# A decoder with routed experts on one Trainium2 core: smaller expert blocks, weights kept in SBUF, and a matrix read at a register's offset

## The chip, the cores and the metric

One core of a Trainium2 chip runs the whole program. Its engines work side by side, each through its own queue in order: TensorE (PE: matmuls, with the loading of the stationary operand shown as PEld), VectorE (DVE), ScalarE (ACT), GpSimd (POOL), and SyncE (SP), which here issues most DMAs. Work passes between them through SBUF and PSUM and is ordered by semaphores. The metric is the device time of one execution in microseconds (us). The trace comes from one profiled execution; its span runs from the first to the last instruction.

## What is computed

A two-layer decoder over 32 sequences of 128 tokens with 128 features, all fp32: 4096 tokens. Only the last step of layer 1 is touched, a mixture of 8 experts of which each token uses the two best:

```python
H, F, E, TOPK = (128, 512, 8, 2)
logits = xf @ router_w + router_b
probs = jax.nn.softmax(logits, axis=-1)
topk_w, topk_i = jax.lax.top_k(probs, TOPK)
topk_w = topk_w / jnp.sum(topk_w, axis=-1, keepdims=True)
...
h = jax.nn.relu(jnp.einsum('th,ehf->tef', xf, w1) + b1)
y = jnp.einsum('tef,efh->teh', h, w2) + b2
out = jnp.einsum('te,teh->th', gates, y)
```

The result is added to the residual stream. Before it come attention, cross attention and gated experts (layer 0), then causal attention and a latent cross attention (layer 1).

## The kernel before

**Order of work.** The program writes the order out by hand as a plan of *schedule slots*. `at(slot, phase, fn)` puts a piece of work in a slot; inside a slot the phases run as open, pre, the attention matmuls, inner, mid, post. Each attention stage takes two slots for each of its 32 sequences, so the three stages fill slots 0 to 191 and end some slots later; `done(stage, g)` is `8 * (8 * stage + g) + 17`, the slot after group g (four sequences) of that stage is finished. Work beside attention is planned relative to it. Each engine gets its instructions in the order of this plan; the sequencers of the engines run through them independently.

**Tokens to slots of a table.** Tokens are treated in two halves (groups 0 to 3 and 4 to 7) of 2048 tokens, 4096 token-expert pairs each. The router (`plan_route`, L1500 to 1690) handles units of eight or four sequences: it normalizes, computes logits on PE (L1571), picks two experts on DVE, counts ranks with matmuls (L1616, L1618), and POOL scatters one row of 130 numbers for each of the two choices (features, the token's row number, its gate) with indirect DMAs (L1644) into a DRAM table `slots[f]` in which each expert has its own room. The last unit is group 7 alone: eight scatters, two in each of slots 230 to 233.

**Blocks.** `expert_blocks` cuts the table of a half into `NB` blocks of `BLOCK` rows of one expert each. The number is fixed: `NB = 2 * HALF // BLOCK + E - 1`, that is 16 + 7 = 23 blocks of 256, whatever the router chooses. `table` (L1735 to L1760, DVE) works out for each block its expert's row in the weights and its first row in the table. For block j:

- `fetch_w` (L1764 to L1769): SP loads the weight row number into a register and issues one DMA of 514 KB, the block's expert's w1, w2 and b1, into one of four buffers `w`.
- `fetch_x` (L1773 to L1778): the same for the block's 256 rows, two to a partition (1040 bytes), into one of ten buffers `bx`.
- `turn`: two PE transposes (L1786) and a DVE copy (L1788) into `bxT`.
- `hidden`: four fp32 products of 256 columns (L1796; each product is two instructions), then bias and relu, two parts on ACT (L1804), two on DVE (L1806).
- `result`: eight fp32 products of 128 columns (L1813), scaled by the gates on ACT (L1821) and DVE (L1823).
- `leave`: two indirect DMAs on POOL (L1828) scatter the rows into `y`, two rows per token.

The order in slot s of block j is: transposes of j + 1, hidden of j, result of j - 1, then the fetches of x for j + 5 and of w for j + 3; the scatter of j - 2 stands between. Half 0's first block is in slot 211 and its last in slot 233, half 1's first in slot 236. In slots 203 to 230 the last groups of the latent attention and the router run beside the blocks; `lkv` (L1098, SP) fetches one sequence's keys each.

**Finish.** `gather` (L1841) reads two rows per token of `y` back, in two DMAs of 256 KB per group, rows of 512 bytes; `finish` adds them on POOL (L1845) and adds the residual on DVE (L1846); `store` (L1485) writes the output. For half 0 this happens beside half 1's blocks, for half 1 after the last block.

At the very end all engines load one word into a register (L1991) to decide whether a general path is needed, which is not taken with these inputs.

Of the kernel before, what the change touches and what calls it, by code (L numbers as in the profile page):

```python
# [22 lines left out]
P = 128  # L23
B, S, D = 32, 128, 128
DC = 96
NG = 4
# [9 lines left out]
ROOM, BLOCK = HALF, 256  # L36
# [3 lines left out]
W_ROW = 512 + 512 + 4  # L40
# [47 lines left out]
def constants():  # L88
# [8 lines left out]
    token = np.tile(np.arange(2 * HALF, dtype=np.int32).reshape(2, B // 2, P).transpose(2, 0, 1), (1, 1, 2))  # L97
# [11 lines left out]
def decoder(ctx: ExitStack, tc: tile.TileContext, a: dict, out: bass.AP):  # L109
# [1054 lines left out]
    def rest_general(y_att, y_mean, flag):  # L1164


        with tc.tile_pool(name="genw", bufs=1) as gw, tc.tile_pool(name="genr", bufs=2) as gp, tc.tile_pool(name="gens", bufs=2) as gs:
# [276 lines left out]
            def relu(x):  # L1444
# [6 lines left out]
                for e in range(E):  # L1451
                    pg = bank(ps_t)
                    nc.tensor.matmul(pg, pick_one[:, e, :], gT, start=True, stop=True)
                    for c in range(4):
                        ph = bank(ps_s)
                        nc.tensor.matmul(ph, w_f[:, e, c * P : (c + 1) * P], xT, start=True, stop=True)
                        h = t([P, NG * P], "fh", 2)
                        nc.scalar.activation(h, ph, AF.Relu, bias=w_f[:, e, 1024 + c : 1025 + c])
                        nc.vector.tensor_tensor(h, pg, h, ALU.mult)
                        nc.tensor.matmul(  # L1460
                            po, w_f[:, e, 512 + c * P : 512 + (c + 1) * P], h, start=False, stop=(e == E - 1 and c == 3)
                        )
# [266 lines left out]
    def expert_blocks(f, total, lazy):  # L1729
# [5 lines left out]
        def table():  # L1735
# [16 lines left out]
            first = row([2, NB], "first")  # L1752
# [5 lines left out]
            nc.vector.tensor_scalar(first[:, 0, :], first[:, 0, :], float(E - 1), float(D), ALU.min, ALU.mult)  # L1758
            where.append(row([2, NB], "where", I32))
            nc.vector.tensor_copy(where[0], first)  # L1760

        def fetch_w(j):
            s = state.setdefault(j, {})
            at_w = nc.values_load(  # L1764
                where[0][:, 0, j : j + 1], engines=[SP], min_val=0, max_val=(E - 1) * D,
                skip_runtime_bounds_check_because="an expert's number, cut off above, by 128",
            )
            s["w"] = lazy["blocks"].tile([P, W_ROW], F32, tag="w", name="w", bufs=4)
            nc.sync.dma_start(s["w"], a["w_f"][bass.ds(at_w, P), :])  # L1769

        def fetch_x(j):
            s = state.setdefault(j, {})
            at_x = nc.values_load(  # L1773
                where[0][:, 1, j : j + 1], engines=[SP], min_val=0, max_val=SLOTS - BLOCK,
                skip_runtime_bounds_check_because="the block's first slot, by the counts of all tokens",
            )
            s["x"] = lazy["blocks"].tile([P, 2, ROW], F32, tag="x", name="bx", bufs=10)
            nc.sync.dma_start(  # L1778
                s["x"].rearrange("p s w -> p (s w)"), slots[f][bass.ds(at_x, BLOCK), :].rearrange("(p s) w -> p (s w)", s=2)
            )  # L1780

        def turn(j):
            s = state[j]
            ps = bank(ps_a)
            for c in range(2):
                nc.tensor.transpose(ps[:, c * P : (c + 1) * P], s["x"][:, c, :D], ident)  # L1786
            s["xT"] = lazy["blocks"].tile([D, BLOCK], F32, tag="xT", name="bxT", bufs=2)
            nc.vector.tensor_copy(s["xT"], ps[:, :BLOCK])  # L1788

        def hidden(j):  # L1790
            s = state[j]
            s["h"] = lazy["blocks"].tile([P, 4, BLOCK], F32, tag="h", name="bh", bufs=2)
            for k in range(2):
                ps = bank(ps_s)
                for c in range(2):
                    nc.tensor.matmul(  # L1796
                        ps[:, c * BLOCK : (c + 1) * BLOCK], s["w"][:, (2 * k + c) * P : (2 * k + c + 1) * P], s["xT"],
                        start=True, stop=True,
                    )
                for c in range(2):  # L1800
                    n = 2 * k + c
                    p, bias = ps[:, c * BLOCK : (c + 1) * BLOCK], s["w"][:, 1024 + n : 1025 + n]
                    if k == 0:
                        nc.scalar.activation(s["h"][:, n, :], p, AF.Relu, bias=bias)  # L1804
                    else:
                        nc.vector.tensor_scalar(s["h"][:, n, :], p, bias, 0.0, ALU.add, ALU.max)  # L1806

        def result(j):
            s = state[j]
            ps = bank(ps_t)  # L1810
            for u in range(2):
                for c in range(4):
                    nc.tensor.matmul(  # L1813
                        ps[:, u * P : (u + 1) * P], s["h"][:, c, u * P : (u + 1) * P],
                        s["w"][:, 512 + c * P : 512 + (c + 1) * P], start=(c == 0), stop=(c == 3),
                    )
            o = s["o"] = lazy["blocks"].tile([P, 2, D], F32, tag="o", name="bo", bufs=4)
            for u in range(2):
                gate = s["x"][:, u, D + 1 : D + 2]
                if u == 0:  # L1820
                    nc.scalar.activation(o[:, u, :], ps[:, u * P : (u + 1) * P], AF.Identity, scale=gate)  # L1821
                else:
                    nc.vector.tensor_scalar(o[:, u, :], ps[:, u * P : (u + 1) * P], gate, None, ALU.mult)  # L1823

        def leave(j):
            s = state.pop(j)
            for u in range(2):
# [256 lines left out]
```

## Time and profile before

| | us |
|---|---|
| median of four runs | 1225.43 |
| lowest and highest | 1221.38, 1226.85 |
| the profiled execution | 1229.21 |
| its span | 1227.4 |

Busy time of each engine in five stretches of the span (us):

| stretch | what runs | PE | DVE | ACT | POOL | granted PE clock | DMA share |
|---|---|---|---|---|---|---|---|
| 933 to 966 | last projections, latent attention, router | 27.80 | 23.32 | 14.53 | 25.17 | 0.79 | 0.38 |
| 966 to 1086 | half 0's blocks beside latent attention and router | 108.00 | 62.32 | 36.73 | 64.42 | 0.94 | 0.42 |
| 1086 to 1113 | end of half 0, last scatters, pause | 18.70 | 9.39 | 5.34 | 17.45 | 0.94 | 0.43 |
| 1113 to 1203 | half 1's blocks | 88.65 | 38.42 | 27.68 | 50.50 | 0.96 | 0.67 |
| 1203 to 1227 | gather, add, store | 0.36 | 3.12 | 0.37 | 8.42 | 0.55 | 0.48 |

How to read the profile's lines: in a timeline, each line has the start and the duration in us, the engine, the source line, the operation, output and inputs, partitions and shape, and the count of instructions merged into it; in brackets the idle time before it and what ended that. In a table by stretches, the columns are length, then busy time and count of PE, PEld, DVE, ACT and POOL, then the granted clock, the DMA share and GB/s. In the answer for one source line, each line has the queue, the operation, the count, and shortest, median and longest duration in ns; a "q" behind an engine's name is its queue's own instruction.

### The profile page before, as it was taken

The page shows a single profiled execution, that of the slowest core. Times are in us where ns is not written, and L with a number is a line of the kernel's source. Part 1 is how long each engine was busy: PE and PEld are TensorE (multiplying, and loading weights), DVE is VectorE, ACT ScalarE, POOL GpSimd, SP SyncE. Part 2 cuts the span into 40 slices and gives each one's busy share as a digit, 9 for nine tenths or more (in the row PEclk, how much of TensorE's full clock was granted, in tenths as well). Part 3 has the DMA queues.
Part 4 walks back from the last instruction along what each step waited for, and adds up shares of the span by engine and source line. Part 5 has one row for each costly group of instructions (what it writes and reads, how often), then busy time and mean ns, then how long its engine had stood idle before and what let it go on. Part 6 is the DMA issues. An engine that isn't in the chain of part 4 may idle for free.

```text
span 1227.4 us, 30561 instructions
## 1 busy us (share of the span) xinstructions
PE 1104.5 (90%) x11877; PEld 822.4 (67%) x11877; DVE 805.2 (66%) x2279; ACT 569.9 (46%) x1299; POOL 639.4 (52%) x911
## 2 busy tenths in 40 slices
PE   3999999999999999999998999989898898887992
PEld 1666666777766667666656666766676687777992
DVE  1578778887778676776676778776676564352441
ACT  2245555577655545545445655644453532321330
POOL 5455445534452454425546664654755456654663
PEclk8599989999999999999999999988987899898996
DMA  7803533002021101110120000001101444445774
GB/s 196 251 8 97 175 97 97 29 27 63 2 46 45 28 19 37 36 36 3 35 47 5 10 15 15 10 11 29 30 16 43 121 145 126 146 148 158 250 237 113
DMA packets 83081, 92.09 MB, mean 75 GB/s; under 512 B 14274, under 2 KB 70264, under 8 KB 82928
## 3 DMA queue, kind: packets, MB, share of 16 engines
q1 hardware_dynamic: 77936, 81.57, 23.2%
q0 software_dynamic: 4992, 8.48, 2.0%
q8 instruction: 96, 1.57, 0.5%
q14 instruction: 57, 0.47, 0.1%
HBM read 53.84 MB, written 38.01 MB: 75 GB/s over the span
## 4 chain that ended last, share of the span: by engine, by line
PE 57%; DVE 14%; POOL 11%; issue 7%; ACT 4%; DMA 4%; SPq 2%; another core or an unknown queue 1%; POOLq 0%; DVEq 0%; ACTq 0%
PE bank L561 15%; PE bank L589 6%; PE bank L1796 4%; DVE msc L564 3%; PE bank L1813 3%; PE bank L871 3%; PE bank L353 2%; POOL y L1828 2%; PE bank L530 2%; PE bank L1143 2%; POOL h L862 2%; DMA g<-spread 2%; PE bank L853 2%; PE bank L1117 1%; PE bank L418 1%
## 5 line engine op out<-in xcount | busy, mean ns | idle before, releaser
L572 ACT ACTIVATE e<-bank 128x512 f32<-128x512 f32 x384 | 207.9, 594 | 239.1 <-PE bank L561 233.1
L564 DVE TENSOR_REDUCE msc<-bank 128x4 f32<-128x512 f32 x384 | 246.3, 683 | 71.7 <-PE bank L561 69.9
L561 PE MATMUL bank<-kb,qz 32*128 32x256 f32 x1536 | 245.4, 418 | 14.4 <-DVE msc L564 14.4
L561 PE MATMUL bank<-qa,kb 32*128 32x128 f32 x3072 | 234.7, 290 | 0.5 <-ACT e L572 0.5
L561 PEld LDWEIGHTS bank<-kb,qz 32*128 32x128 f32 x1536 | 147.6, 192 | 83.9 <-issue 44.1
L561 PEld LDWEIGHTS bank<-qa,kb 32*128 32x128 f32 x3072 | 196.6, 192 | 2.6 <-ACT e L572 1.6
L1828 POOL DMA_INDIRECT y<-bo,bx x92 | 91.7, 996 | 85.9 <-ACT bo L1821 62.7
L575 POOL TENSOR_SCALAR_AFFINE_SELECT e<-e 128x512 f32<-128x512 f32 x128 | 79.6, 646 | 98.5 <-ACT e L572 98.4
L589 PE MATMUL bank<-e,vt 128*32 128x128 f32 x3072 | 127.2, 283 | 3.4 <-POOL e L575 3.1
L1796 PE MATMUL bank<-bxT,w 128*128 128x256 f32 x368 | 92.5, 394 | 3.3 <-issue 1.7
L1813 PE MATMUL bank<-w,bh 128*128 128x128 f32 x736 | 93.8, 282 | 1.2 <-issue 1.2
L1813 PEld LDWEIGHTS bank<-w,bh 128*128 128x128 f32 x736 | 91.1, 198 | 5.3 <-issue 3.8
L589 PEld LDWEIGHTS bank<-e,vt 128*32 128x32 f32 x3072 | 73.3, 110 | 29.3 <-POOL e L575 5.4
L1644 POOL DMA_INDIRECT slots<-rows,r_ati x64 | 63.3, 989 | 31.9 <-issue 16.9
L1796 PEld LDWEIGHTS bank<-bxT,w 128*128 128x128 f32 x368 | 68.9, 198 | 13.1 <-issue 3.0
L862 POOL TENSOR_TENSOR h<-h,g 128x512 f32<-128x512 f32 x30 | 37.6, 1270 | 71.4 <-DVE nm_st L774 35.4
L1806 DVE TENSOR_SCALAR bh<-bank,w 128x256 f32<-128x256 f32 x92 | 40.2, 479 | 41.8 <-PE bank L1796 30.3
L1821 ACT ACTIVATE bo<-bank,bx 128x128 f32<-128x128 f32 x46 | 16.9, 367 | 95.9 <-PE bank L1813 45.9
L1124 ACT ACTIVATE le<-bank,lmx 128x256 f32<-128x256 f32 x64 | 26.8, 471 | 72.1 <-DVE lmx L1123 62.1
L470 DVE SCALAR_TENSOR_TENSOR qa<-bank,head_rows,qz 128x128 f32<-128x128 f32 x192 | 57.6, 342 | 4.0 <-PE bank L462 3.9
L307 ACT ACTIVATE xn<-x,ln_nb,ln_rs 128x128 f32<-128x128 f32 x96 | 41.9, 489 | 38.9 <-POOL ln_nb L301 38.9
L1804 ACT ACTIVATE bh<-bank,w 128x256 f32<-128x256 f32 x92 | 38.5, 470 | 41.0 <-PE bank L1796 20.7
(312 smaller groups left out, 2271.6 us busy)
## 6 DMA issues: line engine op xcount, KB each, us to landing
w<-in_w_f SPq DMA_DIRECT2D x46, 514.0 KB
slots<-nowhere SPq DMA_DIRECT2D x8, 2340.0 KB
g<-spread SPq DMA_DIRECT2D x16, 512.0 KB
bx<-slots SPq DMA_DIRECT2D x46, 130.0 KB
kv<-kcv SPq DMA_DIRECT2D x8, 516.0 KB
lkv<-kv SPq DMA_DIRECT2D x32, 129.0 KB
y<-y SPq DMA_DIRECT2D x16, 256.0 KB
x<-in_x SPq DMA_DIRECT2D x8, 256.0 KB
```

Source lines behind the costliest of these rows:

```text
L307: nc.scalar.activation(m["xn"][:, i, :], X[g][:, i, :], AF.Identity, scale=m["rs"][:, i : i + 1], bias=m["nb"][:, i : i + 1])
L470: nc.vector.scalar_tensor_tensor(s["qa"][:, u, :], s["mp"][:, :P], head_rows[:, 1 - u : 2 - u], m["qz"][:, u, i * P : (i + 1) * P], ALU.mu ...
L561: nc.tensor.matmul(o, l, r, start=start, stop=stop, skip_group_check=True)
L564: nc.vector.tensor_reduce(tops(MSC[bb % 4], 2 * h + j), sc[j].rearrange("p (s n k) -> p s n k", s=2, n=2), AX.X, ALU.max, negate=True)
L572: nc.scalar.activation(e.rearrange("p n q -> p (n q)"), tr[j], AF.Exp, scale=SCALE)
L575: nc.gpsimd.affine_select(out=e, in_=e, compare_op=ALU.is_ge, fill=0.0, base=0, pattern=[[0, 4], [1, P]], channel_multiplier=-1)
L589: nc.tensor.matmul(s3["av"][32 * n : 32 * n + 32, h3 * P : (h3 + 1) * P], m3["vt"][:, i3, h3, n, u, :], es[u][:, n, :], start=(h3 == 0 and ...
L862: engine.tensor_tensor(m["h"][:, c, :], m["h"][:, c, :], m["g"][:, c, :], ALU.mult)
L1644: ins = nc.gpsimd.indirect_dma_start(slots[f], bass.IndirectOffsetOnAxis(ap=m["ati"][:, c, n : n + 1], axis=0), m["rows"][c][:, n, :], Non ...
L1796: nc.tensor.matmul(ps[:, c * BLOCK : (c + 1) * BLOCK], s["w"][:, (2 * k + c) * P : (2 * k + c + 1) * P], s["xT"], start=True, stop=True,)
L1813: nc.tensor.matmul(ps[:, u * P : (u + 1) * P], s["h"][:, c, u * P : (u + 1) * P], s["w"][:, 512 + c * P : 512 + (c + 1) * P], start=(c == ...
L1828: ins = nc.gpsimd.indirect_dma_start(y, bass.IndirectOffsetOnAxis(ap=s["x"][:, u, D : D + 1].bitcast(U32), axis=0), s["o"][:, u, :], None, ...
```

## The change

The block becomes 128 rows, so there are 32 + 7 = 39 blocks per half. One schedule slot takes a pair of blocks, 20 pairs per half, the last with one block. All eight experts' weights are loaded once into SBUF, w1 with b1 (`w1`, 516 columns per expert) and w2 (`w2`, 512 columns per expert), by two DMAs per expert in slots 203 to 210. For each block ACT (first of a pair) or DVE (second) loads a register with the expert's column and copies 516 columns of `w1` into a buffer `w` (four buffers); for w2 PE loads a register and reads the moving operand straight from `w2` at that offset. The x rows come as one row per partition, 128 rows of 520 bytes, a DMA per block. The order of the weights in DRAM changes with it, and the row number of a token in `y` is now `partition * 16 + sequence`, so that `gather` reads a group in one DMA of 512 KB with pieces of 2 KB, into one of two buffers instead of four pairs. Half 0's first pair stays in slot 211, its last falls in slot 230; half 1 begins in the same slot as before.

```diff
-ROOM, BLOCK = HALF, 256
+ROOM, BLOCK = HALF, 128
...
-W_ROW = 512 + 512 + 4
+W1 = 512 + 4
+W_ROW = W1 + 512
...
-    token = np.tile(np.arange(2 * HALF, dtype=np.int32).reshape(2, B // 2, P).transpose(2, 0, 1), (1, 1, 2))
+    token = np.tile(np.arange(2 * HALF, dtype=np.int32).reshape(2, P, B // 2).transpose(1, 0, 2), (1, 1, 2))
...
-            nc.vector.tensor_scalar(first[:, 0, :], first[:, 0, :], float(E - 1), float(D), ALU.min, ALU.mult)
-            where.append(row([2, NB], "where", I32))
+            nc.vector.tensor_scalar(first[:, 2, :], first[:, 0, :], float(E - 1), 512.0, ALU.min, ALU.mult)
+            nc.vector.tensor_scalar(first[:, 0, :], first[:, 0, :], float(E - 1), float(W1), ALU.min, ALU.mult)
+            where.append(row([3, NB], "where", I32))
...
-        def fetch_w(j):
...
-            nc.sync.dma_start(s["w"], a["w_f"][bass.ds(at_w, P), :])
...
+        def value(k, j, engine, top):
+            return nc.values_load(
+                where[0][:, k, j : j + 1], engines=[engine], min_val=0, max_val=top,
...
+        def blocks_of(i):
+            return range(2 * i, min(2 * i + 2, NB))
+
+        def fetch(i):
+            s = state[i] = {"x": [], "w": []}
+            for j in blocks_of(i):
+                at_x = value(1, j, SP, SLOTS - BLOCK)
+                x = lazy["blocks"].tile([P, ROW], F32, tag="x", name="bx", bufs=20)
+                nc.sync.dma_start(x, slots[f][bass.ds(at_x, BLOCK), :])
+                s["x"].append(x)
+
+        def weights(i):
+            for u, j in enumerate(blocks_of(i)):
+                w = lazy["blocks"].tile([P, W1], F32, tag="w", name="w", bufs=4)
+                at_w = value(0, j, (mybir.EngineType.Activation, mybir.EngineType.DVE)[u], (E - 1) * W1)
+                src = lazy["w1"][:, bass.ds(at_w, W1)]
+                if u == 0:
+                    nc.scalar.copy(w, src)
+                else:
+                    nc.vector.tensor_copy(w, src)
+                state[i]["w"].append(w)
...
+        def hidden(i):
+            s = state[i]
+            s["h"] = lazy["blocks"].tile([P, 2, 4, P], F32, tag="h", name="bh", bufs=2)
+            for u, w in enumerate(s["w"]):
+                ps = bank(ps_s)
+                for c in range(4):
+                    nc.tensor.matmul(
+                        ps[:, c * P : (c + 1) * P], w[:, c * P : (c + 1) * P], s["xT"][:, u * P : (u + 1) * P], start=True, stop=True
+                    )
+                for c in range(4):
+                    h, p, bias = s["h"][:, u, c, :], ps[:, c * P : (c + 1) * P], w[:, 512 + c : 513 + c]
+                    if u == 0:
+                        nc.scalar.activation(h, p, AF.Relu, bias=bias)
+                    else:
+                        nc.vector.tensor_scalar(h, p, bias, 0.0, ALU.add, ALU.max)
+
+        def result(i):
...
+            for u, j in enumerate(blocks_of(i)):
+                at_w = value(2, j, mybir.EngineType.PE, (E - 1) * 512)
+                for c in range(4):
+                    nc.tensor.matmul(
+                        ps[:, u * P : (u + 1) * P], s["h"][:, u, c, :], lazy["w2"][:, bass.ds(at_w + c * P, P)],
+                        start=(c == 0), stop=(c == 3),
+                    )
...
-            parts[g] = [lazy["blocks"].tile([P, NG, D], F32, tag=f"y{c}", name=f"y{c}", bufs=4) for c in range(2)]
-            for c in range(2):
-                r = c * HALF + g % (G // 2) * NG * S
-                nc.sync.dma_start(parts[g][c], y[r : r + NG * S].rearrange("(b p) d -> p b d", p=P))
+            b = g % (G // 2) * NG
+            parts[g] = lazy["blocks"].tile([P, 2, NG, D], F32, tag="y", name="yg", bufs=2)
+            nc.sync.dma_start(parts[g], y.rearrange("(c p b) d -> p c b d", c=2, p=P)[:, :, b : b + NG, :])
...
+            def keep(e):
+                def fn():
+                    rows = a["w_f"][e * P : (e + 1) * P]
...
+                    nc.sync.dma_start(lazy["w1"][:, e * W1 : (e + 1) * W1], rows[:, :W1])
+                    nc.sync.dma_start(lazy["w2"][:, e * 512 : (e + 1) * 512], rows[:, W1:])
+                return fn
+
             at(done(2, G - 1) + 2, "open", swap)
+            for e in range(E):
+                at(done(2, G - 1) + 2 + e, "open", keep(e))
...
-                for j in range(3):
-                    at(t - 3 + j, "post", lambda j=j: fetch_w(j))
-                for j in range(5):
-                    at(t, "post", lambda j=j: fetch_x(j))
+                for i in range(4):
+                    at(t, "post", lambda i=i: fetch(i))
+                for i in range(2):
+                    at(t + i, "post", lambda i=i: weights(i))
                 at(t + 1, "post", lambda: turn(0))
...
+                for i in range(pairs):
+                    s = t + 2 + i
+                    if i + 1 < pairs:
+                        at(s, "pre", lambda i=i: turn(i + 1))
+                    at(s, "inner", lambda i=i: hidden(i))
+                    at(s + 1, "post", lambda i=i: result(i))
+                    at(s + 2, "mid", lambda i=i: leave(i))
+                    if i + 4 < pairs:
+                        at(s, "post", lambda i=i: fetch(i + 4))
+                    if i + 2 < pairs:
+                        at(s, "post", lambda i=i: weights(i + 2))
```

## The prediction

> **What bounds the kernel now.** I read the page's totals first, then the busy times in stretches, then PE's timeline over the two expert halves, POOL's beside it, and last the queue instructions of the lines that load registers.
>
> ```profile
> span 1227.4 us, 30561 instructions
> PE 1104.5 (90%) x11877; PEld 822.4 (67%) x11877; DVE 805.2 (66%) x2279; ACT 569.9 (46%) x1299; POOL 639.4 (52%) x911
> ```
>
> PE is busy 90% of the span, but the change touches only what comes after about 940 us, so the shares say little. The second half's blocks run bare, and PE's timeline shows their period:
>
> ```profile
> 1145.66 0.38 PE L1786 MATMUL bank<-ident,bx 128*128 128x128 f32 x2
> 1145.88 1.89 PE L1796 MATMUL bank<-bxT,w 128*128 128x256 f32 x8
> 1147.60 1.95 PE L1813 MATMUL bank<-w,bh 128*128 128x128 f32 x16
> 1149.39 0.38 PE L1786 MATMUL bank<-ident,bx 128*128 128x128 f32 x2
> ```
>
> From one pair of transposes to the next is 3.73 us without an idle stretch: 0.22 + 1.72 + 1.79 by the starts. Every fp32 product is two instructions. One with 256 columns takes 1.72/8 = 0.215 us, one with 128 columns 1.79/16 = 0.112 us: PE's time goes by columns, not by instructions. So here PE bounds; the weight transfers (DMA share 0.67 from 1113 to 1203 us) do not.
>
> Between the halves PE stands still:
>
> ```profile
> 1103.80 3.73 PE L1813 MATMUL bank<-w,bh 128*128 128x128 f32 x32
> 1113.00 0.66 PE L1786 MATMUL bank<-ident,bx 128*128 128x128 f32 x2 [5.47 <-remote]
> 1115.46 3.62 PE L1796 MATMUL bank<-bxT,w 128*128 128x256 f32 x8
> ```
>
> The first block after the pause takes 3.62 us for what takes 1.89 later: the pause also costs clock, some 2.3 us until 1121 us. The pause waits for the x rows of half 1, fetched only after the last scatter of the router on POOL:
>
> ```profile
> 1086.41 0.97 POOL L1644 DMA_INDIRECT slots<-rows,r_ati  x1 [2.87 <-DVE bo L1823]
> 1105.24 0.97 POOL L1644 DMA_INDIRECT slots<-rows,r_ati  x1 [0.30 <-issue]
> ```
>
> Eight scatters of the last unit, two in each of the schedule's slots 230 to 233, lie between the results' scatters of the blocks. The chain of waits adds SP, which sat at L1769 from 1103.98 to 1108.97 for a weight buffer. After the last result (1203.36 us) comes the tail:
>
> ```profile
> 1206.09 0.97 POOL L1828 DMA_INDIRECT y<-bo,bx  x1 [0.30 <-issue]
> 1208.63 3.59 SPq L1841 DMA_DIRECT2D y<-y  x6
> 1221.90 0.69 DVE L1846 TENSOR_TENSOR x<-x,y 128x512 f32<-128x512 f32 x1 [3.30 <-POOL y L1845]
> ```
>
> **Work of the two block sizes.** The number of blocks is fixed by shapes: 23 of 256 slots a half before, 32 + 7 = 39 of 128 after, two to a schedule slot, so 19.5 full slots instead of 23. A full slot after: 2 transposes, 16 hidden and 16 result instructions, all of 128 columns, 34 x 0.1115 = 3.79 us of PE array against 3.73. Bare work per half falls from 23 x 3.73 = 85.8 to 19.5 x 3.79 = 73.9 us.
>
> **What PE's sequencer must do in that slot.** New on PE are two register loads and the address arithmetic of eight dynamic reads. The trace prices each kind, on PE by one sample:
>
> ```profile
> L1991 PEldq TENSOR_LOAD <-word x1: 487/487/487, 1201.2 to 1201.2; - x1
> L1991 ACTq TENSOR_LOAD <-word x1: 479/479/479, 1203.4 to 1203.4; - x1
> L1991 DVEq TENSOR_LOAD <-word x1: 547/547/547, 1221.9 to 1221.9; - x1
> L1778 SPq FUSED_REGOPS  x46: 3/37/722, 959.0 to 1180.2; - x46
> L1778 SPq MOVE bx<-slots x46: 3/29/495, 959.1 to 1180.4; - x46
> ```
>
> PE's load began at 1201.2 us although the last matmuls, ahead of it in program order, started until 1203.1: the sequencer runs about 2 us ahead, and a load of 0.49 us can hide in that. It must keep up on average. Its rate is shown where PE takes the smallest pieces:
>
> ```profile
> 300.00:320.00 20.00, 19.72 (x320) 14.84 (x319) 14.75 (x39) 13.26 (x29) 7.29 (x14) 1.00 0.18 55
> ```
>
> 320 pairs of weight load and matmul in 20 us: at most 62.5 ns each. A new slot needs 34 x 0.0625 = 2.13, two loads 0.97, eight addresses at 0.037 + 0.029 = 0.53, some five semaphore waits of 0.051 = 0.26: 3.89 us, against 3.79 of array. I take 4.0 us for the slot. Bounds: 3.79 if all hides; 3.79 + 0.97 + 0.53 = 5.29 if nothing does.
>
> The Trainium skill gives a price that speaks against the change: "Runtime: NRT & Kernel Launch", section "The ~15µs preamble/postamble breakdown", puts a TENSOR_LOAD at about 1.3 us, a trip to HBM. These loads read SBUF, and the rows above have 0.49; at 1.3 us the sequencer would need 5.5 us a slot and the change would lose.
>
> **The other engines' new work.** ACT copies one weight tile a slot, 128x516: as 128x512 copies there, 0.59, plus 0.48 for its load; with four relus at most 4 x 0.37 and the gate's 0.37 that is 2.9 us. DVE: bxT 0.42, four relus 4 x 0.35, gate 0.35, load 0.55, copy 0.69 (nearest: TENSOR_TENSOR 128x512 0.692; POOL's copy of that size 0.616; two PSUM copies 128x256 0.83): 3.4 us. Both lie under 4.0, and what they make is used two slots later. If DVE's cover goes, its loop is the slot. POOL needs 2 x 1.275 = 2.6 a slot, SP two fetches of 0.70.
>
> On DVE's copy a second rule warns: "SBUF — State Buffer", section "Who interferes with whom", says that such a DVE copy may take the port pair it shares with GpSimd and block it for the whole instruction. No row here has an fp32 copy from SBUF to SBUF on DVE; by the rule scatter issue and copy would delay each other by up to one instruction.
>
> **The sum, part by part.**
>
> 1. *Start, slots 203 to 211.* All weights arrive by 16 DMAs on SP, one expert per slot. SP's waits at L1098 let experts 0 to 6 go by about 952 us, in time. Expert 7's is issued behind the first copies of slot 209, since these read the whole tile at an unknown place, and the next copies wait for it in turn: about 966 + 2 to land, then 0.7, and on DVE bxT of the first block stands behind that. First hidden at about 971 instead of 969.56: +1.5 (0 to +4). Queued behind it on SP are one kv fetch, wanted two slots later, on ACT the relus of slot 211.
> 2. *Half 0, slots 211 to 229.* As many slots as before, each 0.07 longer: 19 x 0.07 = +1.3. Other PE work fills 6.1 us per slot, so the sequencer is covered. Upper bound without cover 19 x 1.56 = +30. Lower: the gaps put to "issue" between 1000 and 1086 us sum to 6.5; if the 514 KB transfers cause them, -6.5.
> 3. *Between the halves.* From the first scatter of the last unit to the first hidden of half 1: 1115.46 - 1086.41 = 29.1. After, half 0 ends three slots sooner, so POOL has 8 scatters and 5 results in a row: the last starts 12 x 1.275 = 15.3 later, releases after 2.5 (as 1206.09 to 1208.63), four fetches of 0.70, landing 2.0, transposes and copy 0.5: 23.1. No weight wait on SP. -6.0 (-8 to 0).
> 4. *Half 1.* 19.5 x 4.0 = 78.0 against 85.8: -7.8 (-11.9 at 3.79, +17.4 at 5.29). The cold start stays.
> 5. *Tail.* The last slot has one block: one scatter of 1.28 less. Gathers: 2 MB as 512 B rows before, 2 KB after, but only two tiles of them, so the third waits for a finish; I work the end out to -0.4. Together -1.7 (-4 to +2).
>
> Sum +1.5 + 1.3 - 6.0 - 7.8 - 1.7 = -12.7. The profiled execution took 1229.21 us (span 1227.4), 3.8 above the median of the four runs, 1225.43; on the median this gives **1212.7 us**.
>
> **The rivals.**
>
> *A, slower: PE's sequencer becomes the bound.* Place: L1813's successor in half 1, where nothing covers. With the loads and addresses bare a slot is 5.29 us: +17.4 in part 4, sum +12.5, **1238 us**. It decides from 19.5x = 85.8 + 4.9, a slot of 4.65 us. For it: 3.89 is already over the array's time, and one sample prices the load. Against: the 2 us of run-ahead. 20%.
>
> *B: DVE's loop is the slot.* 3.4 us plus one blocked instruction of 0.97: 4.4. Part 4 becomes 0, sum -4.9, **1220.5 us**. 18%.
>
> *C, faster: array bound, gaps go.* Parts 1.5, -5.2, -6.0, -11.9, -1.7: -23.3, **1202 us**. For it: the gaps coincide with the stretch of heavy transfers. Against: from 1130 to 1200 us traffic is heavier and there are none. 10%.
>
> *D: the weights are not there in time,* so that the change does not do what it says at its start: if the loads left SP only after 958.3 us, 4.1 MB at the best 250 GB/s shown take 16.5 + 2 us, copies at 977 instead of 964: +13, cancelling the rest: **1225 us**. 7%.
>
> **How the numbers follow.** Forecast 45%, its own range 1207 to 1219. What can be told from no change is about 0.3%, 1221.7 to 1229.1. Faster: 0.43 of the forecast, 0.10 of B, 0.10 of C = 0.63. Same: 0.02 + 0.08 + 0.04 of D = 0.14. Slower: A with what is left of D = 0.23. The range goes from 1203 to 1231: below it half of C, above it most of A's worse part.
>
> **What will show it.** PE's timeline in half 1: 3.8 to 4.1 us from transposes to transposes confirms part 4; gaps between result products next to TENSOR_LOAD on PE's queue mean A; PE idle before hidden, released by DVE, means B. First hidden of half 1 some 23 us after the unit's first scatter confirms part 3. First hidden of half 0 past 975 us means D. A tail over 24 us after the last result refutes part 5. The forecast is wrong if a slot in half 1 takes over 4.65 us or the pause does not shrink.

## The result and the profile after

The changed kernel took 1229.44 us (median of 44 runs) beside 1228.97 us for the kernel before (70 runs): ratio **1.0007**, 95% interval [0.9995, 1.0019]. No change was found where 1212.7 us had been forecast, on a base of 1225.43 us, the median of the first four runs.

First the page's totals of the profile after:

```profile
span 1226.8 us, 31238 instructions
PE 1086.7 (89%) x12007; PEld 815.8 (67%) x12007; DVE 818.6 (67%) x2365; ACT 599.2 (49%) x1401; POOL 624.4 (51%) x897
```

PE has 17.8 us less to do, yet the span is 0.6 us shorter. PE's timeline in half 1 shows that the blocks did get cheaper:

```profile
1140.61 0.38 PE L1797 MATMUL bank<-ident,bx 128*128 128x128 f32 x2
1140.83 1.95 PE L1807 MATMUL bank<-bxT,w 128*128 128x128 f32 x16
1142.62 1.95 PE L1824 MATMUL bank<-all_w,bh 128*128 x16
1144.40 0.38 PE L1797 MATMUL bank<-ident,bx 128*128 128x128 f32 x2
```

A slot takes 1144.40 - 1140.61 = 3.79 us, without an idle stretch: the array's time and nothing else. The answer for the line that loads registers, and that of the result's line in half 1, show what PE does beside it:

```profile
L1765 PEldq TENSOR_LOAD <-tb_where x78: 295/300/492, 975.6 to 1195.1; - x78
```

```profile
L1824 PEldq FUSED_REGOPS  x156: 42/46/46, 1126.9 to 1196.3; - x156
```

A load takes 0.30 us (median), an address 0.046, and both are hidden.

Marks in the timelines cut the span into five: the first hidden product of half 0, the last unit's first scatter, the first hidden of half 1, the end of the last result, the end of the span. Two pairs of profiles are cut in this way: the first, and one of two later runs of the same kernels on two chips (experiments f1 and g1 below), in which PE stands without a reason that the profile shows for 0.2 us at most. Lengths in us:

| stretch | before | after | difference | before (g1) | after (f1) | difference |
|---|---|---|---|---|---|---|
| up to half 0 | 969.6 | 966.1 | -3.5 | 968.9 | 970.3 | +1.5 |
| half 0 | 116.9 | 132.6 | +15.8 | 104.6 | 109.5 | +4.9 |
| pause | 29.0 | 23.3 | -5.7 | 23.1 | 23.0 | -0.1 |
| half 1 | 87.9 | 76.0 | -11.9 | 87.0 | 75.2 | -11.8 |
| tail | 24.1 | 28.8 | +4.7 | 24.5 | 28.8 | +4.4 |
| span | 1227.4 | 1226.8 | -0.6 | 1208.1 | 1206.9 | -1.2 |

What half 1 gains is given back in half 0 and in the tail, and the pause gives nothing in the second pair. The start's -3.5 in the first pair is chance: the same kernel begins half 0 at 966.1, 969.4 and 970.3 us (after, e1, f1). The first pair's half 0 has something else in it. PE's timeline of the profile after:

```profile
1053.93 1.36 PE L1824 MATMUL bank<-all_w,bh 128*128 x8
1056.44 0.59 PE L1824 MATMUL bank<-all_w,bh 128*128 x2 [1.16 <-issue]
1057.85 1.10 PE L1824 MATMUL bank<-all_w,bh 128*128 x4 [0.82 <-issue]
1059.30 0.79 PE L1824 MATMUL bank<-all_w,bh 128*128 x2 [0.35 <-issue]
1060.01 0.37 PE L1797 MATMUL bank<-ident,bx 128*128 128x128 f32 x1
1061.44 0.45 PE L1797 MATMUL bank<-ident,bx 128*128 128x128 f32 x1 [1.05 <-issue]
```

PE waits for nothing that the profile shows, and gets a few products every 0.7 or 1.4 us; meanwhile and afterwards the clock is low as well. Such *stands* sum to 8.3 us here and to 7.7 us before, in other places. They had to be told apart from what the change costs.

The tail, from SP's timeline of the profile after:

```profile
1205.10 0.87 SPq L1850 DMA_DIRECT2D yg<-y  x2
1211.95 0.38 SPq L1486 DMA_DIRECT2D out_x<-x  x1
1212.43 0.45 SPq L1850 DMA_DIRECT2D yg<-y  x1
1212.97 0.45 SPq L1486 DMA_DIRECT2D out_x<-x  x1
1213.52 0.51 SPq L1850 DMA_DIRECT2D yg<-y  x1
```

Two gathers go out at once, the third and fourth 7.3 and 8.4 us later, after the finishes that free their buffers, each behind a store of such a group.

### The profile page after: what moved, and what is told of

It reads as the page before. It is cut to its first block, busy times and chain, and to the rows that moved or that the text cites. A ratio compares the mean times of both kernels' runs of the same rounds, so it can differ in the third digit from the quotient of the medians.

```text
span 1226.8 us, 31238 instructions
## 1 busy us (share of the span) xinstructions
PE 1086.7 (89%) x12007; PEld 815.8 (67%) x12007; DVE 818.6 (67%) x2365; ACT 599.2 (49%) x1401; POOL 624.4 (51%) x897
## 4 chain that ended last, share of the span: by engine, by line
PE 57%; DVE 15%; POOL 10%; issue 6%; DMA 5%; ACT 4%; SPq 1%; another core or an unknown queue 1%; POOLq 0%; DVEq 0%; ACTq 0%
PE bank L562 14%; PE bank L590 6%; PE bank L1807 5%; PE bank L1824 4%; DVE msc L565 3%; PE bank L872 3%; PE bank L354 2%; DMA g<-spread 2%; POOL h L863 2%; PE bank L1144 2%; PE bank L531 2%; PE bank L1118 1%; PE bank L854 1%; POOL slots L1645 1%; PE bank L419 1%
## 5 line engine op out<-in xcount | busy, mean ns | idle before, releaser
L562 PE MATMUL bank<-qa,kb 32*128 32x128 f32 x3072 | 230.7, 288 | 0.0
L562 PEld LDWEIGHTS bank<-qa,kb 32*128 32x128 f32 x3072 | 193.2, 191 | 0.9 <-issue 0.7
L1838 POOL DMA_INDIRECT y<-bo,bx x78 | 77.4, 992 | 90.0 <-ACT bo L1831 50.6
L1807 PE MATMUL bank<-bxT,w 128*128 128x128 f32 x624 | 84.8, 290 | 5.2 <-issue 3.3
L1824 PE MATMUL bank<-all_w,bh 128*128 x624 | 83.5, 288 | 2.7 <-issue 2.6
L1807 PEld LDWEIGHTS bank<-bxT,w 128*128 128x128 f32 x624 | 80.2, 206 | 7.2 <-issue 5.0
L1824 PEld LDWEIGHTS bank<-all_w,bh 128*128 128x128 f32 x624 | 78.2, 202 | 5.7 <-issue 5.3
L1815 DVE TENSOR_SCALAR bh<-bank,w 128x128 f32<-128x128 f32 x152 | 42.7, 344 | 36.4 <-PE bank L1807 18.9
L1813 ACT ACTIVATE bh<-bank,w 128x128 f32<-128x128 f32 x160 | 45.8, 370 | 33.2 <-PE bank L1807 24.0
L298 POOL TENSOR_SCALAR ln_rs<-ln_mv 128x4 f32<-128x4 f32 x24 | 5.5, 229 | 90.5 <-DVE ln_mv L293 90.0
```

The source lines that it names most:

```text
L562: nc.tensor.matmul(o, l, r, start=start, stop=stop, skip_group_check=True)
L1807: nc.tensor.matmul(ps[:, c * P : (c + 1) * P], w[:, c * P : (c + 1) * P], s["xT"][:, u * P : (u + 1) * P], start=True, stop=True)
L1813: nc.scalar.activation(h, p, AF.Relu, bias=bias)
L1824: nc.tensor.matmul(ps[:, u * P : (u + 1) * P], s["h"][:, u, c, :], lazy["w2"][:, bass.ds(at_w + c * P, P)], start=(c == 0), stop=(c == 3),)
L1838: ins = nc.gpsimd.indirect_dma_start(y, bass.IndirectOffsetOnAxis(ap=x[:, D : D + 1].bitcast(U32), axis=0), s["o"][:, u, :], None, bounds_ ...
```

## The experiments

Ratios are to the kernel before on the same chip. The changed kernel is the base unless another is named. Later kernels are built on earlier ones.

### Does PE's sequencer cost anything? (e2, e3, e4)

e2 reads w2 at a place fixed in the program, so not the weights of the block's own expert:

```diff
-                at_w = value(2, j, mybir.EngineType.PE, (E - 1) * 512)
...
-                        ... lazy["w2"][:, bass.ds(at_w + c * P, P)],
+                        ... lazy["w2"][:, j % E * 512 + c * P : j % E * 512 + (c + 1) * P],
```

> The changed kernel, with w2 read at a place fixed in the program (the block's number modulo 8) and so without the 78 register loads and their address arithmetic on PE; the weights are not the block's own, all else is as in the changed kernel. Theory 1 (register loads and addresses cost PE's sequencer its run-ahead in half 0): half 0's stretch falls from 132.6 to 118 to 122 us and the ratio to before to about 0.989. Theory 2 (it is the number of PE's instructions, 34 pairs a slot instead of 26): it falls by 3 us at most, ratio 0.998 to 1.0007. Theory 3 (chance in one execution, or contention with transfers): no change of the ratio. Half 1's slot stays at 3.79 us in all.

Ratio 0.9993 [0.9969, 1.0017]. Half 0 took 108.4 us and half 1 75.1; with the register loads they took 109.5 and 75.2 (f1). By these profiles all of PE's loads and addresses cost some 1 us at most, so theory 1 falls.

e3, the kernel before with the hidden products in halves:

```diff
-                    nc.tensor.matmul(ps[:, c * BLOCK : (c + 1) * BLOCK], ..., s["xT"], ...)
+                    for v in range(2):
+                        nc.tensor.matmul(ps[:, c * BLOCK + v * P : c * BLOCK + (v + 1) * P], ...,
+                            s["xT"][:, v * P : (v + 1) * P], ...)
```

> The kernel before, with the hidden products cut into 128 columns, so that a block takes 34 pairs of weight load and matmul as in the changed kernel and nothing else is altered. Theory 2 (number of PE's instructions): the stretch of half 0 grows from 116.9 by 8 to 16 us, ratio 1.007 to 1.014 (half 1's block may add 0.06 us each, 1.4 us in all). Theory 1 (register loads): under 3 us, ratio 1.000 to 1.003.

Ratio 1.0010 [0.9983, 1.0037], half 0 104.1 us (104.6 in g1). Theory 2 falls too: the number of PE's instructions does not set half 0's length.

e4, the kernel before with two `nc.values_load(..., engines=[PE])` ahead of each block's results:

> The kernel before, with two register loads a block on PE, ahead of the result's products, whose values nothing uses. Theory 1 (register loads stop PE's sequencer in half 0): the stretch of half 0 grows from 116.9 by 8 to 16 us, ratio 1.007 to 1.014. Theory 2 (number of PE's instructions): under 2 us, ratio 1.000 to 1.002. In half 1 the block keeps 3.73 us by all theories, as the changed kernel's loads were hidden there.

Ratio 1.0012 [0.9990, 1.0034], half 0 103.0 us. This is a miss: the trace has 92 semaphore instructions on that line and no register load, presumably since nothing used the values. It is only another look at the kernel before; the verdict on the loads rests on e2.

### The tail (e1)

```diff
-            parts[g] = lazy["blocks"].tile([P, 2, NG, D], F32, tag="y", name="yg", bufs=2)
+            parts[g] = lazy["blocks"].tile([P, 2, NG, D], F32, tag="y", name="yg", bufs=4)
```

> The changed kernel, with four buffers for the gathers instead of two. If the tail grew because the third and fourth gather wait for a finish, the time from the end of the last result to the end of the span falls from 28.8 to about 24 us, and the ratio to before falls by about 0.004, to 0.997. If the tail grew for the gathers' new form (512 KB in one DMA), it stays at 28 to 29 us. Nothing is edited before the tail, so the stretch from the first hidden of half 0 to the first scatter of the last unit is a repeat of the changed kernel: 130 to 135 us if its 132.6 us (116.9 before) belongs to the change, under 125 if it was chance in one execution.

Ratio 0.9969 [0.9949, 0.9989]; tail 24.6 us. Half 0 took 109.7 us, so what the first profile has above that was not the change's. SP's timeline of e1:

```profile
1184.00 1.38 SPq L1850 DMA_DIRECT2D yg<-y  x3
1190.07 0.38 SPq L1486 DMA_DIRECT2D out_x<-x  x1
1190.55 0.45 SPq L1850 DMA_DIRECT2D yg<-y  x1
```

Three gathers go out together; the last still stands behind a store in SP's queue. So the buffers cost the tail: with four, the gather's new form takes what the old one took (24.5 us in g1). The tail shows this; the ratio alone would not, since the changed kernel itself has 0.9975 on a chip of this kind (f1).

### Stands that no wait explains (f1, g1)

The kernels unchanged, on two chips. First the changed one:

> The changed kernel itself. If the chip shows no unexplained stands: half 0's stretch 108 to 110 us, pause 23 us, half 1 75 to 76 us, tail 28 to 29 us, ratio 0.999 to 1.002. If the stands are there: half 0's stretch 120 to 135 us with 6 to 10 us of idle on PE put to issue, the ratio the same.

Ratio 0.9975 [0.9956, 0.9993], below the expected 0.999 to 1.002; the stretches came as expected. PE's idle put to "issue" after 960 us is 0.2 us. Then the kernel before:

> The kernel before itself, ratio 1.000. Without unexplained stands: from first hidden of half 0 to the last unit's first scatter 103 to 104 us, pause 23 to 24 us with 4 to 5 us of stand on PE, half 1 87.5 us, tail 24 us, and no half clock between 10 and 35 us after half 0's start. With them: half 0's stretch 115 to 125 us and a pause of 25 to 30 us.

Ratio 1.0006 [0.9976, 1.0035], no stands, pause 23.1 us. Two lines of the expectation missed: half 0 took 104.6 us, and a half clock of 3.4 us did follow, 24.5 us after half 0's start.

Over all profiles: on three chips, where the kernel before took 1208 to 1211 us, ten profiles have 0 to 0.2 us of stands after 960 us; where it took 1229, all ten have 6 to 17 us, whichever the kernel. So the stands belong to the chip or its state at that time, not to the change. They are not PE's alone. In e10 (below), PE's timeline from 1097 us on and the answer for SP's fetch line from 1100 to 1112 us:

```profile
1097.82 0.71 PE L1824 MATMUL bank<-all_w,bh 128*128 x4
1099.23 0.27 PE L1824 MATMUL bank<-all_w,bh 128*128 x1 [0.69 <-issue]
1099.95 0.37 PE L1824 MATMUL bank<-all_w,bh 128*128 x1 [0.46 <-issue]
1102.10 0.37 PE L1824 MATMUL bank<-all_w,bh 128*128 x1 [1.77 <-issue]
```

```profile
L1781 SPq MOVE bx<-slots x6: 3/29/698, 1103.3 to 1111.1; - x6
L1781 SPq FUSED_REGOPS  x6: 3/37/699, 1104.2 to 1111.9; - x6
```

Register moves on SP with a median of 29 ns take up to 698 at the same time; in f4, without stands, none takes more than 37 (1080 to 1100 us). What holds both queues was not found.

### DVE's load and the clock in half 0 (e5, e8, e9, f3)

Without stands, more than half of half 0's excess sits in its first four slots. From the first hidden to the hidden of slot 215, the changed kernel (the first, f1), those that differ only elsewhere (e1, e6) and e2 took 31.4 to 31.6 us; the kernel before, with nothing else altered in that stretch (the first, e4, g1, g2) or with split products (e3), 27.2 to 30.2.

e8 gives the kernel before the DVE work of the changed one:

```diff
+            if j > 0:
+                more = lazy["blocks"].tile([P, 516], F32, tag="more", name="more", bufs=2)
+                nc.vector.tensor_copy(more, state[j - 1]["w"][:, :516])
...
-                        nc.vector.tensor_scalar(s["h"][:, n, :], p, bias, 0.0, ALU.add, ALU.max)
+                        for v in range(2):
+                            q = slice(v * P, (v + 1) * P)
+                            nc.vector.tensor_scalar(s["h"][:, n, q], p[:, q], bias, 0.0, ALU.add, ALU.max)
```

> The kernel before, with what the changed kernel adds on DVE and nothing else: a copy of 128x516 a block (from the block's weight tile into a buffer that nothing reads) and its two relu instructions cut into four. Theory 4: DVE's residual add of slot 214 comes 0.6 us later, PE stands about 2 us instead of 1.4 and its clock falls: the step from hidden 214 to hidden 215 grows from 10.25 to 13 to 13.6 us, the stretch of half 0 from 103 to 105 to 108, ratio 1.002 to 1.005. Rival (what costs is in the changed kernel's PE work): the step grows by no more than 0.7 us and the ratio stays at 1.000 to 1.002. Half 1's block keeps 3.73 us in both.

Ratio 1.0025 [0.9997, 1.0053], 31.1 us to slot 215. PE's timelines, first of e4 (the kernel before, in effect), then of e8:

```profile
990.79 0.21 PE L1112 MATMUL bank<-masked,ident_b 32*128 32x128 bf16 x1 [1.39 <-DVE x L1087]
990.93 0.70 PE L1117 MATMUL bank<-lkv,lqT 64*128 64x256 f32 x4
991.56 2.05 PE L1817 MATMUL bank<-w,bh 128*128 128x128 f32 x16
```

```profile
988.61 0.21 PE L1112 MATMUL bank<-masked,ident_b 32*128 32x128 bf16 x1 [1.97 <-DVE x L1087]
988.75 1.07 PE L1117 MATMUL bank<-lkv,lqT 64*128 64x256 f32 x4
989.75 3.28 PE L1818 MATMUL bank<-w,bh 128*128 128x128 f32 x16
```

The bracket grows from 1.39 to 1.97 us, the changed kernel's own value, and the same 16 products then take 3.28 instead of 2.05 us at half the clock. DVE's work alone makes the same wait. That it makes the same loss is not shown. The step with the stand takes 12.67 us, less than the 13 expected; it takes 10.24 in e4, but 11.84 in g1 and 11.81 in g2, the kernel before with DVE's work as it was. Another 1.6 us of e8's excess over e4 come two slots earlier, from a half clock that g2 has too. Half 0 as a whole took 122.5 us with its stands, and the ratio allows both theories.

e5 (on e1) takes the copy off DVE:

```diff
-                if u == 0:
-                    nc.scalar.copy(w, src)
-                else:
-                    nc.vector.tensor_copy(w, src)
+                nc.scalar.copy(w, src)
```

> The changed kernel with four gather buffers, and both weight copies of a pair on ACT instead of one on ACT and one on DVE. Theory 4 (half 0 loses at one place: in slot 214 DVE is a queue without a gap, the weight copy and two more relu instructions put its residual add 0.6 us later, PE then stands 1.97 us instead of 1.39, and its clock is halved for 6.8 us): the step from hidden 214 to hidden 215 falls from 13.5 to 10.3 to 11 us, the stretch of half 0 from 109.7 to 105 to 107, the ratio to before from 0.997 to 0.993 to 0.995. Rival (the clock falls there for what PE itself does, or the register loads on ACT and DVE are the cost): 13 us or more, ratio 0.996 or higher. Half 1's slot stays 3.79 us if ACT's two copies, four relus and gate (some 3.8 us with loads) fit; if not it grows and costs up to 0.3 us a slot, 6 us.

Ratio 0.9976 [0.9950, 1.0001]. A miss: the stand shrank to 1.63 us, but the clock fell all the same, 31.4 us to slot 215, 12.33 of them in the step that was to take 10.3 to 11. Half 0 took 132.0 us, with stands of 8.0. Half 1 took 76.2 us, against 76.0 in the first profile after.

e9 and f3 (on e7 below) also move one relu, `if u == 0 or (f == 0 and c == 0)`:

> As e7_both, and in half 0 one of DVE's four relu instructions of a pair goes to ACT, so that DVE's work in a slot is that of the kernel before. Theory 4, sharpened (PE's stand before slot 215 decides on its clock: 1.39 us in three profiles without a dip, 1.97 us in five profiles all with one, 1.63 us in two profiles, one with and one without): the stand falls to 1.35 to 1.45 us and no half clock follows within 30 us of half 0's start; from first hidden to the hidden of slot 215 27 to 28.3 us, where the kernels with a dip took 31.1 to 31.6. Rival (the dips come from elsewhere, the stand is only beside them): 31 us again. The ratio moves by less than 0.003, 0.9935 to 0.9965.

> The kernel of e9_relu_moved. By theory 4 PE stands 1.37 us before slot 215 and its clock does not fall in the 30 us after half 0's start: 28 to 28.7 us from first hidden to the hidden of slot 215. Ratio at or up to 0.003 under f2_both_again; e9_relu_moved's 1.0009 was then the stands' doing. If the ratio is again 0.003 or more over f2_both_again, the relu on ACT costs something that the clock's gain does not pay.

Inconclusive. e9: stand 1.37 us, no half clock there, 28.6 us, as theory 4 says, but ratio 1.0009 [0.9990, 1.0028], worse than e7's. f3: PE stood 0.76 us on the moved relu instead, the clock fell, 32.0 us; ratio 0.9878 [0.9854, 0.9902] beside f2's 0.9889. And in g1 and g2 the clock fell after 1.39 us, which is one reason why g2 reaches 30.2. So a stand of 1.96 or 1.97 us was followed by half the clock in all six profiles that have it, but a shorter one does not keep the clock up for sure, and this repair is not shown to work.

What decides after shorter stands stays open. The half clocks in these traces last 3.41 us or a multiple of it, up to 34.1 in f4, so the clock's changes lie on a grid of 3.41 us. The Trainium skill, "TensorE: Matmul & The Clock Gate", section "What's actually happening", has the activity window at about 3.4 us and says that it runs free of the program; so the same stand can fall into one window or be cut by two. Laid on the grid, the traces fit this only in part. Of three stands of 1.62 or 1.63 us, e7's is cut (0.99 and 0.63 us) and the clock stayed; those of e5 and f2 lie whole in one window and it fell. But all five stands of 1.39 us lie whole, and it fell after two. And in seven profiles (e2, e5, e6, e8, f2, f3, g2) it fell for 3.4 us some 10 us after half 0's start, though the profile shows PE busy without a gap in the 3.4 us before. The same page's section "HAM oscillation — how this bites in real kernels" tells one to avoid idle gaps of PE of more than about 3.4 us; here it fell after gaps of 1.97 us, and in those seven profiles after none; the measurement decides.

### The pause: what PE waits for (e6, e7, f2, g2)

PE's timelines of g1 and of f1:

```profile
1086.51 3.73 PE L1813 MATMUL bank<-w,bh 128*128 128x128 f32 x32
1094.96 0.66 PE L1786 MATMUL bank<-ident,bx 128*128 128x128 f32 x2 [4.72 <-DMA bx<-slots]
```

```profile
1082.45 1.16 PE L1824 MATMUL bank<-all_w,bh 128*128 x8
1099.96 0.48 PE L1797 MATMUL bank<-ident,bx 128*128 128x128 f32 x1 [16.35 <-DMA bx<-slots]
```

The changed kernel's half 0 ends three slots sooner and PE stands 16.35 instead of 4.72 us. It waits for rows behind the last unit's scatters, which come when attention and router get there. Three lines of POOL's timeline of f1 show what is mixed in with them:

```profile
1082.63 0.97 POOL L1838 DMA_INDIRECT y<-bo,bx  x1 [0.30 <-issue]
1083.91 0.97 POOL L1838 DMA_INDIRECT y<-bo,bx  x1 [0.30 <-DVE tb_where L1762]
1085.19 1.12 POOL L1645 DMA_INDIRECT slots<-rows,r_ati  x1 [0.30 <-issue]
```

e6 (on e1) sends the eight scatters first; e7 is e5 and e6 together, and f2 is e7 on a chip without stands:

```diff
+                    if groups == UNITS[-1]:
+                        at(t + 8, "pre", scatter(c, k))
+                    else:
+                        at(t + 8 + n // 2, ("pre", "inner")[n % 2], scatter(c, k))
-                    at(t + 8 + n // 2, ("pre", "inner")[n % 2], scatter(c, k))
```

> The changed kernel with four gather buffers, and the last unit's eight router scatters all in its first slot, ahead of the results' scatters of slots 230 to 232 on POOL. If POOL's queue sets the pause between the halves: the time from the first scatter of the last unit to the first hidden of half 1 falls by the five results' scatters that stood between, 5 x 1.275 = 6.4 us, from 23.0 to about 16.6, and the ratio from 0.997 to 0.9915 to 0.993. If the pause is set by SP's fetches, or by the result tiles that come free later: 20 us or more, ratio 0.995 or higher.

> The changed kernel with four gather buffers, both weight copies on ACT, and the last unit's scatters first. If both causes stand and add: ratio 0.987 to 0.990. If only one of them stands: 0.991 to 0.995.

> The kernel of e7_both (four gather buffers, both weight copies on ACT, last unit's scatters first). Without unexplained stands: the pause is 16.5 to 17 us instead of the 20.0 seen before, half 0's stretch 105 to 109 us, tail 24.7 us, and the ratio is 0.988 to 0.992. With them: pause 20 us, ratio 0.994 to 0.999 as before.

e6: ratio 0.9971 [0.9941, 1.0000], pause 20.7 us. e7: 0.9964 [0.9937, 0.9991], pause 20.0. Both missed: SP crawled through the fetches just then, with register moves of up to 0.70 us. f2: **0.9889** [0.9851, 0.9928], pause 16.4 us, as worked out. Half 0 took 108.5 us (109.5 in f1) and the tail 25.7 (28.8), so of the gain over f1 some 6.6 us are the pause, 3 the buffers, and the copies on ACT bring 1 at most.

g2 makes the same edit in the kernel before:

> The kernel before, with the last unit's eight scatters all in its first slot, ahead of the results' scatters. If the move's gain needs the change (blocks of half 0 end three slots sooner, so PE stands 16 us and the scatters are what it waits for): here PE's stand of 4.7 us is all that can go, then it is held by half 0's own blocks, and the ratio is 0.996 to 0.999. Rival (the move brings the kernel before the same 6 us): 0.993 to 0.996.

Ratio 0.9984 [0.9962, 1.0006], pause 20.6 us: PE's stand falls from 4.72 to 2.44 us, and half 0's own blocks hold it after that: the last scatter starts at 1079.37 us, but SP, waiting for weight buffers that results free, sends the first x fetch of half 1 at 1086.30. The move pays where the change has emptied the pause.

### Half 0 three slots later (e10, e11, e12, f4)

```diff
-            begins = [done(2, G // 2 - 1) + 40, done(2, G - 1) + 33]
+            begins = [done(2, G // 2 - 1) + 43, done(2, G - 1) + 33]
```

e10 is e7 with this line, e11 has the moved relu as well, e12 is the changed kernel with this line alone, and f4 is e10 on the chip of f2:

> As e7_both, and half 0's blocks begin three slots later, so that their last pair stands in slot 233 again. Theory 5 (the three slots that half 0 saves go into a longer stand of PE before half 1, 16 us where the kernel before had 5 to 6, for the first scatter of the last unit comes when attention and router get there, not when the blocks are done): three pairs' products, 3 x 3.8 us, move from ahead of that scatter into the stand; the ratio falls from 0.9964 by 0.005 to 0.009, to 0.987 to 0.991 (0.005 if a slot without a block still takes 3.5 us for attention's own chain), and PE's stand falls from 9.5 to under 4 us. Rival (the stand is not usable, for POOL's queue or the result tiles hold the last pairs, and half 1 starts later by as much): 0.995 or higher.

> As e10_later, with one relu of a pair moved from DVE to ACT in half 0 as well. Theories 4 and 5 together: 0.001 to 0.003 under e10_later. If DVE's load no longer meets the clock there, because the blocks stand beside other slots of attention: the same as e10_later within 0.001.

> The changed kernel with nothing altered but half 0's blocks three slots later. Theory 5: the ratio falls from the changed kernel's 1.0007 to 0.992 to 0.996, as the stand of PE before half 1 (16.4 us) takes in some 11 us of products; the time from the first scatter of the last unit to the first hidden of half 1 stays at 23 us, the stretch from the first hidden of half 0 to that scatter loses three slots. Rival (the stand is not usable): 0.999 or higher. Tail 28 to 29 us in both, as in the changed kernel.

> The kernel of e10_later. Theory 5 without unexplained stands: PE's stand before half 1 is under 4 us and the ratio is 0.004 to 0.009 under f2_both_again. Rival (half 1 starts later by as much as half 0's last pairs take): the same ratio as f2_both_again within 0.002. With unexplained stands: 15 us or more of them, ratio 0.998 to 1.002.

e10 0.9994 [0.9964, 1.0025], e11 1.0008 [0.9982, 1.0033], e12 1.0013 [0.9988, 1.0037]: nothing won, and 15.6 to 17.2 us of stands on PE, twice the others'. Of these, 4 to 9 us fell between the first scatter and half 1, where PE now works, so these three decide nothing. f4, without stands: **0.9837** [0.9804, 0.9870], 1191.47 us beside 1210.76. PE's timeline there:

```profile
1089.30 1.95 PE L1824 MATMUL bank<-all_w,bh 128*128 x16
1091.09 1.06 PE L1807 MATMUL bank<-bxT,w 128*128 128x128 f32 x8
1091.98 2.84 PE L1824 MATMUL bank<-all_w,bh 128*128 x24
1094.66 0.38 PE L1797 MATMUL bank<-ident,bx 128*128 128x128 f32 x2
1095.56 0.77 PE L1797 MATMUL bank<-ident,bx 128*128 128x128 f32 x2 [0.52 <-DVE bxT L1799]
1097.66 0.60 PE L1807 MATMUL bank<-bxT,w 128*128 128x128 f32 x3 [1.33 <-ACT w L1789]
```

The long wait is gone: half 0's last pairs run where PE stood 9.5 us in f2. So the stand can be used. What that wins is less sure. Against f2 the ratio is lower by 0.0052, within the theory's 0.004 to 0.009, but the two intervals overlap (0.9851 to 0.9870), and f3's reaches as far. In the profiled executions half 1 starts at 1097.7 us, against 1098.7 in f2 and 1096.9 in f3: the first scatter comes 2.5 us sooner than in f2, not three slots, and the pause is 17.9 instead of 16.4 us. One price that the theory left out is in the trace: with the slots ahead of half 0 emptied, the granted clock is at half from 969.7 to 1003.8 us, 34.1 us, where f2 has 13.7 us of it between 970.0 and 1004.1 us. f4 has the lowest median here, on a chip without stands; on a chip with them no gain was seen.

## Why the prediction was wrong

Step by step, forecast against the pair without stands:

1. **Start, +1.5.** Right in number: the 1.07 us wait of PE that lies 6.9 us before the first hidden in g1 lies 8.2 us before it in f1, +1.3. The weights were there, so D is out. But the wait that the step names, for expert 7's weights, is not seen: in f1 DVE's copy ahead of `bxT` follows DVE's other work at 969.03 us without idle time. Instead PE waits 1.23 us for DVE's `lon`, which it does not in g1. That the sizes agree is luck.
2. **Half 0, +1.3.** Mis-sized: +4.9. "Other PE work fills 6.1 us per slot, so the sequencer is covered" was right about the sequencer (e2). But DVE and ACT were costed only for half 1. In half 0 DVE also does attention's and the router's work, and its 0.6 us of additional work comes out as a wait of PE (e8). Of the 4.9 us, 2.7 come before the hidden of slot 215: 1.7 in the step with that wait, 0.9 in the first, where f1's clock stays low longer. That the longer wait is what brings the clock down is argued, not shown, and the cause of the other 2.2 us is open. The first pair's +15.8 is mostly stands.
3. **Pause, -6.0.** One of the two steps that failed. The 23.1 us worked out for the changed kernel is exactly its time (23.0). The base was wrong: 29.1 us was one execution with stands in and ahead of the pause, and without them the kernel before also takes 23.1 (g1, e4). In the first pair the pause falls by 5.7, which looks like a hit; without stands it falls by 0.1. Three slots less of half 0 were counted as time won where PE only waits longer; POOL's queue sets that end in both kernels. In g1 it runs 8 scatters and 6 results without a gap, 16.7 us from the first scatter to the last, in f1 8 and 5, 15.7 us. The queue of 13 was read rightly, and the same sum for the kernel before could have told so.
4. **Half 1, -7.8.** Right in kind, too small: -11.8. The sum 3.89 us added each instruction's duration on the sequencer as if nothing overlapped, with a load of 0.49 where the median is 0.30; with 0.30 it gives 3.51, less than the array's 3.79 us, which was the answer. A, and B in half 1, are refuted; C was right about half 1 alone.
5. **Tail, -1.7.** The other step that failed, wrong in sign: +4.4. That "the third waits for a finish" was seen, but no price for it stands in the sum. The third and fourth gather leave 7.3 and 8.4 us late, and with four buffers the tail falls from 28.8 to 24.6 us (e1). That is the length before (24.5), so the scatter less brought nothing either.

Together the forecast was -12.7 and the pair without stands gives -1.2; 6 of the difference is the pause, 6 the tail, 4 half 0, less 4 in half 1. That pair comes from two chips. On the chip of f1, the changed kernel is 3.05 us faster by the medians (ratio 0.9975), where the first comparison has 1.0007; that stands hid some 3 us there is possible, but was not separated.

## What to carry to other kernels

Before a stretch of the old profile is counted as a saving, ask how much of it one execution added by chance: idle time put to "issue" is a sign, and a second profile, on another chip if possible, settles it. When a stage gets shorter, follow what its end waits for; if another chain sets it, the time comes out only after work is moved, here by sending the scatters first. Starting the stage later as well used the wait, but what it wins is not settled. A buffer count that is cut is a wait: on the last chain, waits of 7 to 8 us cost 4.2 us here.

## What was not expected of the hardware

- The same kernel before took 1208 to 1211 us on three chips and 1229 elsewhere, there with PE and SP getting their instructions some 0.7 us apart for stretches of up to some 10 us (e10). Its cause is open.
- A fp32 copy of 128x516 from SBUF to SBUF took 0.43 us on DVE and 0.62 on ACT.
- PE's register loads, 0.30 us each, cost nothing that can be seen in half 1, even with PE's array busy without a gap: 75.2 us with them (f1), 75.1 without (e2).
- The granted clock fell to half for 3.4 us in seven profiles although the profile shows PE busy without a gap in the 3.4 us before; in g2 PE was then at small products, such as the router's with 8 columns. Its cause is open.
